# Value weights of a graph-attention kernel by two levels of Strassen's algorithm

## The chip, the cores and the metric

The kernel runs on one core of a Trainium2 chip. The core has five engines that work side by side: TensorE (PE in the profile; PEld is its loading of weights), VectorE (DVE), ScalarE (ACT), GpSimd (POOL) and SyncE (SP, which here only issues DMAs). Each engine runs its instructions in the order in which the program gives them, and waits in that order. Matrix products go to PSUM, eight banks of 512 float32 columns; POOL does not touch PSUM here, so results are moved out ("evicted") by DVE or ACT. The metric is device time in microseconds, the median of three runs.

## The reference, cut to what matters

Two graph layers over x (128 graphs of 64 nodes, 768 features), all in float32:

```python
# layer 0
u = einsum('bld,bmd->blm', x, x) / sqrt(768)
attn = softmax(u) * adj, renormalized
h_left, h_self, h_right = x @ W_left.T + b_left, x @ W_self.T + b_self, x @ W_right.T + b_right
ctx = upper(attn) @ h_left + diag(attn)[..., None] * h_self + lower(attn) @ h_right
x = layernorm(x + relu(layernorm(ctx) * gamma + beta))
# layer 1, 12 heads of 64
q, k, v = x @ Wq + bq, x @ Wk + bk, x @ Wv + bv
scores = q k^T / 8 + beta * adj, masked where adj is 0
x = layernorm(x + softmax(scores) @ v)
```

The change is in `v = x @ Wv + bv` alone.

## The kernel before, in words

The 8192 tokens go in 16 blocks of 512 (`NBLK`). The loop over n works on layer 1 of block n and layer 0 of block n + 1 in turns, in five stages whose order PE follows: the left and right parts of layer 0 of the next block (from block 3 on together, `both_sides`), its self part (`self_part`), the values of block n (`values`), and three projections of queries and keys (`projected`, hg = 0, 1, 2). Smaller work (attention of layer 0, scores, weighted sums, the context pieces of 8 matmuls) is put between products by hooks: a dictionary from a place in a stage to functions that are called there. Element-wise work waits in three queues, `first`, `urgent` and `lazy`; after each product `step` takes an item from them, and a call with `light` set takes none of the ordinary DVE items (those without a kind). The whole loop is scheduled by hand: the order of the program is the order on each engine.

Every projection is done by one level of Strassen's algorithm in Winograd's form: the 512 x 768 block and the 768 x 768 matrix are cut in four, and seven products replace eight. `combined` and `combined4` form the sums of tokens S (POOL), `prepare` formed the sums of weights at the start and stored them in DRAM. `seven` runs the seven products, in the order 1, 2, 6, 5, 7, 4, 3, for two halves j of the tokens: 14 places, three matmuls of 128 x 128 weights by 384 columns in each, so 42 for a stage. The products gather in PSUM tiles X (1, 6, 7, 4) and Y (2; 5, 3), two of each, and are evicted on the way (14 evictions). `by_tokens` is this with the tokens as PE's stationary operand and a weight piece of 128 x 384 as the moving one, loaded by SP into the ring `wst` (19 buffers).

From block 3 on, `both_sides` uses two levels (`nested`): each of the seven products is again done by seven, over the left and right matrices side by side (384 columns). A pair of numbers, first level and second level, names a product. `ORDER2` is the first-level order 7, 1, 2, 6, 5, 4, 3; the order on PE is 7.1 7.2, then for each i: i.6 i.5 i.7, the next one's 1 and 2, i.4 i.3. Products 2, 5, 4 and 3 of the second level take two matmuls, the others one. Each product of the second level is evicted by itself (49 evictions): `middle` takes it to a temporary U, `final` to its quarter of the output, in both cases adding what is there already. At first-level product 5, POOL adds c22 to c21, the bias to c12 and c12 to c22, quarter by quarter (lines 450 to 458). `second_level` forms the second-level sums of tokens of one product by four POOL instructions in a tile q (lines 341 to 344) of a pool of two buffers; `blk["S"]["deep"]` holds the first two, formed in `combined` for layer 0 of blocks from 3 on. `deepened` makes the 63 second-level matrices of left and right in blocks 0 and 1 and stores them in `lr_d`.

The stage of values, in which the change lies, begins when the self part ends. Its hooks: place 0, the last sum of tokens and the loads for later transposes; places 1, 3, 5, 7, the four context pieces, each 8 matmuls and two DVE instructions on them; place 6, six DVE transposes of 512 columns put in `urgent` (`turned`, line 310); places 9 and 13, small steps of a layernorm. The sums of tokens for the values are formed in the self part, place 11.

Of the kernel before, what the change touches and what calls it, by code (L numbers as in the profile page):

```python
# [11 lines left out]
F32 = mybir.dt.float32  # L12
AF = mybir.ActivationFunctionType
ALU = mybir.AluOpType
# [3 lines left out]
P = 128  # L18
# [28 lines left out]
MATRICES = (1, 2, 8, 3, 9, 5, 7, 4, 6)  # L47
DEEP = 3
# [3 lines left out]
def gnn_two_layers(ctx: ExitStack, tc, x, adj, wl, bl, ws, bs, wr, br, gamma, beta,  # L52
# [9 lines left out]
    s2_p = ctx.enter_context(tc.tile_pool(name="s2", bufs=2))  # L62
# [3 lines left out]
    wst = ctx.enter_context(tc.tile_pool(name="wst", bufs=19))  # L66
# [218 lines left out]

    def transposed(src, xT, t):

        for c0 in range(0, KC, 3):
            ps = ps_mm.tile([P, 4, P], F32, tag="mm", name="ps_x")
            for c in range(3):  # L290
                nc.tensor.transpose(ps[:, c, :], src[:, c0 + c :: KC], ident)  # L291
            nc.scalar.copy(xT[:, c0 : c0 + 3, t * P : (t + 1) * P], ps[:, 0:3, :])
# [132 lines left out]
    def nested(width, sums, load, multiply, view, C, bias0, bias1, hooks):  # L425
# [9 lines left out]

        def part(i, q):
            return bias0(q[1]) if i == 1 else old[i][q] if i in old else None

        def taken(i, q, ps, dst, add):
            if add is None:  # L440
                nc.scalar.copy(dst, view(ps))
            else:
                nc.vector.tensor_tensor(dst, view(ps), add, ALU.add)  # L443
# [16 lines left out]
        def sub(i, j):  # L460
            for place in range(28):
                if place * 49 // 28 == len(done):
                    for f in hooks.get(place, ()):
                        f()
# [6 lines left out]
            multiply(F[i], W[i], j, ps)  # L471
# [13 lines left out]

            step(len(done) > 8, j in (5, 1, 4))
# [4 lines left out]
        for k, i in enumerate(ORDER2):  # L491
            after = ORDER2[k + 1] if k + 1 < len(ORDER2) else None
            if after:
                F[after], W[after] = sums(after), load(after)
            for j in (6, 5, 7):
                sub(i, j)
            if after:
                sub(after, 1)
                sub(after, 2)
            for j in (4, 3):  # L500
                sub(i, j)
# [118 lines left out]
    def both_sides(n, hooks):  # L620
# [6 lines left out]
        def sums(i):  # L627
            return blk["S"]["deep"].get(i) or second_level(blk["S"][i])

# [7 lines left out]
        def multiply(F, w, j, ps):  # L637
            f, last = F
            fs = [(f[j], w[j])]
            if j in (2, 5, 4, 3):  # L640
                fs.append((last[{2: 1, 5: 2, 4: 2, 3: 3}[j]], w[8 if j in (2, 4) else 9]))
            for k, (a, b) in enumerate(fs):
                nc.tensor.matmul(ps, lhsT=a, rhs=b, start=(k == 0 and j in (1, 2, 5)), stop=(k == len(fs) - 1),  # L643
                                 skip_group_check=True)

        def view(ps):
# [4 lines left out]
        nested(HALF, sums, load, multiply, view, C,  # L651
               lambda b: bias_lr[:, :, b * QUAD : (b + 1) * QUAD],
               lambda b: bias_lr[:, :, HALF + b * QUAD : HALF + (b + 1) * QUAD], hooks)
# [112 lines left out]
    def values(n, hooks={}, stay=False):  # L766
# [12 lines left out]
        by_tokens("v", blocks[n]["S"], last, None, hooks)  # L779
# [240 lines left out]
    for n in range(NBLK):  # L1020
# [12 lines left out]
        for i, (when, hooks, place) in zip(ORDER2, ((0, val, 2), (0, val, 8), (0, qk[0], 8), (0, qk[1], 6),  # L1033
                                                    (0, qk[2], 6), (1, own, 3), (1, val, 3))):
            if when == n:
                begin, steps = deepened(i)
                at(hooks, place, begin)
                at(hooks, place + 3, lambda i=i, steps=steps: urgent.extendleft([(("d", i), *f) for f in reversed(steps)]))

# [14 lines left out]
        if not last:  # L1054
            if n > 0:
# [29 lines left out]
                def sums1():  # L1085
                    settle(("t1", n))
                    blocks[n]["S"] = combined(blocks[n]["xT"])

                at(own, 11, sums1)
# [47 lines left out]
        else:  # L1137
            transposed1(n)
            at(qk[0], 9, lambda: later(("m", n), *mask(n), queue=urgent))
# [142 lines left out]
```

## Time and profile before

| what | time, us |
|---|---|
| median of three runs | 2923.98 (2923.8 to 2925.47) |
| profiled execution | 2923.8, its span 2922.1 |
| PE busy | 2872.4 (98% of the span) |
| DVE busy | 1979.6 (68%) |
| ACT busy | 1120.4 (38%) |
| POOL busy | 732.2 (25%) |
| DMA | 613.18 MB, 210 GB/s over the span |

The page's first part gives each engine's busy time; the chain that ended last follows the work back from the last instruction. In a timeline a line is start, length, engine, source line, operation, output and inputs, shape, number of instructions merged, and in brackets how long the engine had been idle and for what. The granted PE clock is full in all slices of the span.

### The profile page before, as it was taken

To read this page: it belongs to the slowest core of one execution; us is meant where nothing else is said; L and a number is where in the kernel's file an instruction comes from. 1 tells how busy PE (TensorE), PEld (TensorE's weight loads), DVE (VectorE), ACT (ScalarE), POOL (GpSimd) and SP (SyncE) were. 2 spreads that over 40 slices of the span, in tenths; PEclk is the share of its full clock that TensorE was granted. 3 is DMA by queue.
4 is the path that set the end of the run, shared out by engine and by line. 5 is a ranking of instruction groups with operands and counts; after the bars stand their busy time and mean duration, and the time that the engine had idled before them with its cause. 6 is when DMAs were issued, how large, how long until landed. Compare 5 with 4: busy or idle time off the path is not lost.

```text
span 2922.1 us, 49871 instructions
## 1 busy us (share of the span) xinstructions
PE 2872.4 (98%) x17578; PEld 1931.7 (66%) x17578; DVE 1979.6 (68%) x3973; ACT 1120.4 (38%) x2107; POOL 732.2 (25%) x879
## 2 busy tenths in 40 slices
PE   9999999999999999999999999999999999999997
PEld 5658566585665857657576675766757567585685
DVE  6778777676676766757667576766767667676655
ACT  0005224354243443434444334343434424354255
POOL 3133123213042140412405123051230512314110
PEclk9999999999999999999999999999999999999999
DMA  9788877859577595875958669486694956849443
GB/s 340 231 272 272 251 214 202 243 143 286 153 207 238 160 274 149 226 220 167 270 145 246 195 181 267 137 269 174 184 260 138 285 160 195 246 139 288 140 127 100
DMA packets 440662, 613.18 MB, mean 210 GB/s; under 512 B 53584, under 2 KB 416720, under 8 KB 440416
## 3 DMA queue, kind: packets, MB, share of 16 engines
q1 hardware_dynamic: 362960, 495.93, 56.5%
q10 hardware_dynamic: 60848, 44.05, 8.0%
q0 software_dynamic: 16608, 70.01, 6.6%
q8 instruction: 143, 2.34, 0.3%
q14 instruction: 103, 0.84, 0.1%
HBM read 539.43 MB, written 77.27 MB: 211 GB/s over the span
## 4 chain that ended last, share of the span: by engine, by line
PE 93%; ACT 3%; POOL 2%; DVE 1%; issue 1%; DMA 0%; POOLq 0%; SPq 0%; ACTq 0%
PE ps_X L389 36%; PE ps_Y L389 27%; PE ps_Y L643 11%; PE ps_X L643 10%; PE ps_ctx L682 3%; ACT eT L853 2%; PE sc L833 2%; PE ps_y L882 2%; PE u L532 2%; POOL q L342 1%; ACT L853 1%; ACT uqk L801 1%; PE ps_x L291 0%; POOL q L341 0%; POOL q L343 0%
## 5 line engine op out<-in xcount | busy, mean ns | idle before, releaser
L389 PE MATMUL ps_X<-xT,wqk 128*128 128x256 f32 x1728 | 395.8, 381 | 9.5 <-ACT uqk L801 9.5
L853 ACT ACTIVATE eT<-s 32x256 f32<-32x256 f32 x768 | 317.8, 414 | 172.4 <-DVE s L862 162.4
L389 PEld LDWEIGHTS ps_X<-xT,wqk 128*128 128x128 f32 x1728 | 325.8, 190 | 67.0 <-ACT uqk L801 16.2
L322 POOL TENSOR_TENSOR S<-hT 128x768 f32<-128x768 f32 x16 | 28.9, 1807 | 1132.7 <-PE ps_Y L389 1102.1
L389 PE MATMUL ps_Y<-S,wqk 128*128 128x256 f32 x1152 | 264.3, 379 | 0.0
L687 ACT ACTIVATE unused<-o 128x768 f32<-128x768 f32 x60 | 50.6, 844 | 499.6 <-DVE o L684 346.1
L389 PEld LDWEIGHTS ps_Y<-S,wqk 128*128 128x128 f32 x1152 | 218.9, 190 | 29.8
L443 DVE TENSOR_TENSOR lr<-ps_Y,u_deep 128x384 f32<-128x384 f32 x273 | 152.1, 557 | 109.1 <-PE ps_Y L643 83.4
L643 PE MATMUL ps_Y<-wlr,q 128*128 128x384 f32 x546 | 208.5, 491 | 0.0
L389 PE MATMUL ps_X<-wv,xT 128*128 128x384 f32 x576 | 195.5, 489 | 0.0
L801 ACT ACTIVATE uqk<-ps_X,bq 128x256 f32<-128x256 f32 x144 | 68.1, 473 | 325.0 <-PE ps_X L389 323.9
L809 DVE TENSOR_TENSOR q<-ps_Y,uqk 128x256 f32<-128x256 f32 x144 | 61.0, 424 | 177.5 <-ACT uqk L801 89.3
L389 PE MATMUL ps_X<-ws,hT 128*128 128x384 f32 x540 | 179.2, 486 | 0.0
L643 PE MATMUL ps_X<-wlr,q 128*128 128x384 f32 x364 | 151.0, 497 | 14.6 <-POOL q L342 6.0
L389 PEld LDWEIGHTS ps_X<-wv,xT 128*128 128x128 f32 x576 | 108.0, 190 | 80.4 <-issue 8.4
L892 DVE SCALAR_TENSOR_TENSOR o<-ps_y,rz,o 128x64 f32<-128x64 f32 x720 | 154.7, 278 | 6.4
L443 DVE TENSOR_TENSOR u_deep<-ps_X,lr 128x384 f32<-128x384 f32 x195 | 107.5, 551 | 68.2 <-PE ps_X L643 66.6
L389 PEld LDWEIGHTS ps_X<-ws,hT 128*128 128x128 f32 x540 | 102.5, 190 | 71.4
L643 PEld LDWEIGHTS ps_Y<-wlr,q 128*128 128x128 f32 x546 | 101.6, 190 | 67.2
L420 DVE TENSOR_TENSOR u<-ps_X,bv 128x384 f32<-128x384 f32 x96 | 53.4, 557 | 132.5 <-PE ps_X L389 132.5
L389 PE MATMUL ps_X<-S,wqk 128*128 128x256 f32 x576 | 138.2, 385 | 0.0
L389 PE MATMUL ps_Y<-xT,wqk 128*128 128x256 f32 x576 | 135.6, 385 | 0.0
(258 smaller groups left out, 5471.6 us busy)
## 6 DMA issues: line engine op xcount, KB each, us to landing
wlr<-lr_d SPq DMA_DIRECT2D x819, 192.0 KB, 3.5
wqk<-qk_d SPq DMA_DIRECT2D x672, 192.0 KB, 2.4
wv<-d_v SPq DMA_DIRECT2D x192, 192.0 KB, 2.7
ws<-d_s SPq DMA_DIRECT2D x180, 192.0 KB, 5.8
wv<-in_L_gnn_Wv_dram SPq DMA_DIRECT2D x144, 192.0 KB, 4.1
ws<-in_L_gnn_W_self_dram SPq DMA_DIRECT2D x135, 192.0 KB, 5.4
xa<-in_x_dram SPq DMA_DIRECT2D x64, 384.0 KB, 5.3
sq<-in_x_dram ACTq DMA_DIRECT2D x56, 384.0 KB, 7.7
```

Source lines behind the costliest of these rows:

```text
L389: nc.tensor.matmul(ps, lhsT=a, rhs=b, start=(c == 0 and i in (1, 2, 5)), stop=(c == len(fs) - 1), skip_group_check=True)
L420: recent["u"] = evicted[nm] = nc.vector.tensor_tensor(u, ps, bias[nm][:, b * HALF : (b + 1) * HALF], ALU.add)
L443: nc.vector.tensor_tensor(dst, view(ps), add, ALU.add)
L532: nc.tensor.matmul(u[g * L : (g + 1) * L, t, :], lhsT=xT[:, c, tok], rhs=xT[:, c, tok], start=(c == 0), stop=(c == KC - 1))
L643: nc.tensor.matmul(ps, lhsT=a, rhs=b, start=(k == 0 and j in (1, 2, 5)), stop=(k == len(fs) - 1), skip_group_check=True)
L682: nc.tensor.matmul(ps[g * L : (g + 1) * L, 0:HALF], lhsT=blk["aT"][:, t, g * L : (g + 1) * L], rhs=blk["lr"][t][:, g, cols], start=True, s ...
L801: nc.scalar.activation(u, ps, AF.Identity, bias=bias["qk"[j]][:, c : c + 1])
L809: nc.vector.tensor_tensor(dst, ps, part, ALU.add)
L833: nc.tensor.matmul(sc[r][g * L : (g + 1) * L, t, c, :], lhsT=q[rows, c, tok], rhs=k[rows, c, tok], start=True, stop=True)
L853: nc.scalar.activation(e[to[0], :, to[1]], pairs[rows, :, cols], AF.Exp)
L882: nc.tensor.matmul(y[r, h][cols, t, c, :], lhsT=eT[rows, 2 * h + t, c, cols], rhs=v[rows, 2 * h + t, g, hg + c * HC, :], start=True, stop= ...
L892: nc.vector.scalar_tensor_tensor(res[:, r, c, hg, :], ps[:, t, c, 0:HD], rz[:, t, c : c + 1], res[:, r, c, hg, :], ALU.mult, ALU.add)
```

## The change

From block 3 to block 14 the values are computed by two levels too; blocks 0 to 2 and the last keep one level.

- `deepened_values` makes the second-level matrices of Wv in block 2 and stores them in `v_d`, in five pairs to a first-level product (`PAIRS`). A column half is cut by the parity of the head, so the loads read runs of 64 columns.
- `nested` is made general: `applied` does the one or two matmuls of a product; `places` is 28 for both sides and 14 for values. With 14, all evictions are DVE's, and ordinary DVE items of the queues run only after a second-level product 7.
- The pool of q has three buffers instead of two, the ring of weights 17 instead of 19. In both users of `nested`, the second-level sums of products 4 and 3 are now formed together, before 5.6; those of the others one product ahead, as before.
- The sums of tokens for the values are formed at place 10 instead of 11 of the self part, with the two first sets of second-level sums among them.
- The second half of the values' bias is replaced by its difference to the first half at block 3, and loaded anew for the last block.

```diff
...
 MATRICES = (1, 2, 8, 3, 9, 5, 7, 4, 6)
+PAIRS = ((1, 2), (8, 6), (5, 9), (7, 4), (3,))
 DEEP = 3
...
     s_p = ctx.enter_context(tc.tile_pool(name="s_p", bufs=1))
-    s2_p = ctx.enter_context(tc.tile_pool(name="s2", bufs=2))
+    s2_p = ctx.enter_context(tc.tile_pool(name="s2", bufs=3))
     l0 = ctx.enter_context(tc.tile_pool(name="l0", bufs=1))
...
     tmp = ctx.enter_context(tc.tile_pool(name="tmp", bufs=2))
-    wst = ctx.enter_context(tc.tile_pool(name="wst", bufs=19))
+    wst = ctx.enter_context(tc.tile_pool(name="wst", bufs=17))
     st = ctx.enter_context(tc.tile_pool(name="st", bufs=2))
...
         return begin, [(partial(formed, 0),), (partial(formed, 1),), (end, "gap")]
+    v_d = tc.dram_tile([7, len(PAIRS), P, 2, QUAD], F32, name="v_d")
+    def deepened_values(i):
+        src, w = pieces["v"][i], {}
+        place = {m: v_d[i - 1, k, :, j, :].rearrange("p (j d) -> p j d", d=HD)
+                 for k, pair in enumerate(PAIRS) for j, m in enumerate(pair)}
+        def half(k, h):
+            return src[:, k, :].rearrange("p (j r d) -> p r j d", r=2, d=HD)[:, h]
+        def heads(a):
+            return a.rearrange("p (j d) -> p j d", d=HD)
+        def begin():
+            for k in range(2):
+                w[k] = wst.tile([P, 2, QUAD], F32, tag="w", name="w_deep")
+                for h in range(2):
+                    nc.sync.dma_start(out=heads(w[k][:, h, :]), in_=half(k, h))
+            for m, k, h in ((1, 0, 0), (2, 1, 0), (8, 2, 0), (3, 1, 1), (9, 2, 1)):
+                nc.gpsimd.dma_start(out=place[m], in_=half(k, h))
+        def formed():
+            b11, b12, b21, b22 = (w[k][:, h, :] for k in range(2) for h in range(2))
+            for out, a, b in ((b11, b12, b11), (b12, b22, b12), (b22, b22, b11), (b21, b21, b22)):
+                nc.vector.tensor_tensor(out, a, b, ALU.subtract)
+        def end():
+            for m, k, h in ((5, 0, 0), (7, 0, 1), (4, 1, 0), (6, 1, 1)):
+                nc.gpsimd.dma_start(out=place[m], in_=heads(w[k][:, h, :]))
+        return begin, [(formed,), (end, "gap")]
...
-    def nested(width, sums, load, multiply, view, C, bias0, bias1, hooks):
+    def applied(F, w, j, ps):
+        f, last = F
+        fs = [(f[j], w[j])]
+        if j in (2, 5, 4, 3):
+            fs.append((last[{2: 1, 5: 2, 4: 2, 3: 3}[j]], w[8 if j in (2, 4) else 9]))
+        for k, (a, b) in enumerate(fs):
+            nc.tensor.matmul(ps, lhsT=a, rhs=b, start=(k == 0 and j in (1, 2, 5)), stop=(k == len(fs) - 1),
+                             skip_group_check=True)
+    def nested(width, S, load, view, C, bias0, bias1, hooks, places):
...
+        def sums(i):
+            return S["deep"].get(i) or second_level(S[i])
         def part(i, q):
...
         def taken(i, q, ps, dst, add):
-            if add is None:
+            if add is None and places == 28:
                 nc.scalar.copy(dst, view(ps))
+            elif add is None:
+                nc.vector.tensor_copy(dst, view(ps))
             else:
...
         def sub(i, j):
-            for place in range(28):
-                if place * 49 // 28 == len(done):
+            for place in range(places):
+                if place * 49 // places == len(done):
                     for f in hooks.get(place, ()):
...
             ps = (X if j in (1, 6, 7, 4) else Y)[i][:, 0:width]
-            multiply(F[i], W[i], j, ps)
+            applied(F[i], W[i], j, ps)
             if j == 1:
...
                 final(i, (0, 1), ps, U[i, 2])
-            step(len(done) > 8, j in (5, 1, 4))
+            step(places == 14 or len(done) > 8, j in (5, 1, 4) if places == 28 else j != 7)
...
             if after:
-                F[after], W[after] = sums(after), load(after)
+                W[after] = load(after)
+            for later_one in (ORDER2[k + 1 :] if i == 5 else (after,) if i != 4 and after else ()):
+                F[later_one] = sums(later_one)
             for j in (6, 5, 7):
...
-        def sums(i):
-            return blk["S"]["deep"].get(i) or second_level(blk["S"][i])
         def load(i):
...
-        def multiply(F, w, j, ps):
-            f, last = F
-            fs = [(f[j], w[j])]
-            if j in (2, 5, 4, 3):
-                fs.append((last[{2: 1, 5: 2, 4: 2, 3: 3}[j]], w[8 if j in (2, 4) else 9]))
-            for k, (a, b) in enumerate(fs):
-                nc.tensor.matmul(ps, lhsT=a, rhs=b, start=(k == 0 and j in (1, 2, 5)), stop=(k == len(fs) - 1),
-                                 skip_group_check=True)
         def view(ps):
...
                        for a in range(2) for b in range(2)} for m in range(2) for n_ in range(2)}
-        nested(HALF, sums, load, multiply, view, C,
+        nested(HALF, blk["S"], load, view, C,
                lambda b: bias_lr[:, :, b * QUAD : (b + 1) * QUAD],
-               lambda b: bias_lr[:, :, HALF + b * QUAD : HALF + (b + 1) * QUAD], hooks)
+               lambda b: bias_lr[:, :, HALF + b * QUAD : HALF + (b + 1) * QUAD], hooks, 28)
...
-        by_tokens("v", blocks[n]["S"], last, None, hooks)
+        def load(i):
+            w = {}
+            for k, pair in enumerate(PAIRS):
+                two = wst.tile([P, 2, QUAD], F32, tag="w", name="wv2")
+                nc.sync.dma_start(out=two[:, 0 : len(pair), :], in_=v_d[i - 1, k, :, 0 : len(pair), :])
+                w.update({m: two[:, j, :] for j, m in enumerate(pair)})
+            return w
+        def heads(a):
+            return a.rearrange("p (j d) -> p j d", d=HD)
+        if n < DEEP or stay:
+            by_tokens("v", blocks[n]["S"], last, None, hooks)
+        else:
+            C = {(m, h): {(a, k): v[:, 2 * m + a, k, h * HC : (h + 1) * HC, 0:HD]
+                          for a in range(2) for k in range(2)} for m in range(2) for h in range(2)}
+            nested(QUAD, blocks[n]["S"], load, lambda ps: heads(ps[:, 0:QUAD]), C,
+                   lambda k: pairs(bias["v"][:, 0:HALF])[:, k], lambda k: pairs(bias["v"][:, HALF:D])[:, k], hooks, 14)
         if not stay:
...
                 at(hooks, place + 3, lambda i=i, steps=steps: urgent.extendleft([(("d", i), *f) for f in reversed(steps)]))
+        for i, (hooks, place) in zip(ORDER2, ((left, 3), (left, 9), (right, 3), (right, 9), (own, 2), (own, 7), (val, 5))):
+            if n == 2:
+                begin, forms = deepened_values(i)
+                at(hooks, place, begin)
+                at(hooks, place + 2, lambda i=i, forms=forms: urgent.extendleft([(("dv", i), *f) for f in reversed(forms)]))
+        if n == DEEP:
+            settle("dv")
+            at(left, 0, lambda: nc.vector.tensor_tensor(bias["v"][:, HALF:D], bias["v"][:, HALF:D],
+                                                        bias["v"][:, 0:HALF], ALU.subtract))
...
                     settle(("t1", n))
-                    blocks[n]["S"] = combined(blocks[n]["xT"])
-                at(own, 11, sums1)
+                    blocks[n]["S"] = combined(blocks[n]["xT"], n)
+                at(own, 11 if n < DEEP else 10, sums1)
                 at(val, 0, lambda: combined4(blocks[n]["S"]))
...
             transposed1(n)
+            at(qk[0], 0, lambda: nc.sync.dma_start(out=bias["v"], in_=bv.partition_broadcast(P)))
             at(qk[0], 9, lambda: later(("m", n), *mask(n), queue=urgent))
...
```

## The prediction

> **What bounds the kernel now.** I read the page's busy shares first, then the chain that ended last, then the merged chain in order of time, and last the timelines of one block (the one that runs from about 1969 to 2149 us).
>
> ```profile
> PE 2872.4 (98%) x17578; PEld 1931.7 (66%) x17578; DVE 1979.6 (68%) x3973; ACT 1120.4 (38%) x2107; POOL 732.2 (25%) x879
> PE 93%; ACT 3%; POOL 2%; DVE 1%; issue 1%; DMA 0%; POOLq 0%; SPq 0%; ACTq 0%
> L389 PEld LDWEIGHTS ps_X<-xT,wqk 128*128 128x128 f32 x1728 | 325.8, 190 | 67.0 <-ACT uqk L801 16.2
> ```
>
> PE is 98% busy and is 93% of the chain, so time is passes times their price. Each f32 matmul is two records ("passes"): the 42 matmuls of a block's self part are 84 records.
>
> The merged chain gives the price (start, length, what):
>
> ```profile
> 30.82 7.74 PE ps_X L389 x24
> 240.99 5.18 PE ps_X L389 x24
> ```
>
> 24 passes over 384 columns take 7.74 us, 322.5 ns each; 24 over 256 take 5.18, 215.8 each. So 106.7 ns per 128 columns, and by that line a pass over 192 columns costs 322.5 - 1.5 x 106.7 = 162.5 ns.
>
> The value stage of the block, in PE's timeline:
>
> ```profile
> 1995.24 2.10 PE L389 MATMUL ps_X<-wv,xT 128*128 128x384 f32 x6
> 1997.26 1.51 PE L682 MATMUL ps_ctx<-lr,aT 128*64 128x384 f32 x8
> 1998.70 2.20 PE L389 MATMUL ps_X<-wv,xT 128*128 128x384 f32 x6
> ...
> 2028.88 2.75 PE L389 MATMUL ps_X<-xT,wqk 128*128 128x256 f32 x12
> ```
>
> It lasts 2028.88 - 1995.24 = 33.64 us without a wait: 84 passes are 27.09, and the four context pieces the other 6.55.
>
> How the nested form behaves is seen where it already runs, in the both-sides stage. First the handing of X between PE and DVE (all engines' timeline):
>
> ```profile
> 2111.28 1.22 DVE L862 TENSOR_TENSOR s<-s,mx 128x1024 f32<-128x1024 f32 x1
> 2111.29 1.53 POOL L342 TENSOR_TENSOR q<-q,S 128x128 f32<-128x128 f32 x1
> 2112.42 0.55 DVE L443 TENSOR_TENSOR u_deep<-ps_X,lr 128x384 f32<-128x384 f32 x1
> 2113.07 0.88 PE L643 MATMUL ps_X<-wlr,q 128*128 128x384 f32 x2 [0.46 <-POOL q L342]
> 2113.99 0.56 DVE L443 TENSOR_TENSOR u_deep<-ps_X,lr 128x384 f32<-128x384 f32 x1 [1.02 <-PE ps_X L643]
> ```
>
> The wait of 0.46 is put down to POOL, but PE moves 0.10 us after the eviction ends at 2112.97. DVE starts 0.27 after the stream ends (2113.07 + 0.645 = 2113.72, then 2113.99). So X is lost to PE for 0.27 + eviction + 0.10. Second, POOL's queue at product 5 (POOL's timeline):
>
> ```profile
> 2125.49 0.99 POOL L457 TENSOR_TENSOR lr<-lr,bias_lr 128x384 f32<-128x384 f32 x1 [0.29 <-DVE rz L888]
> 2126.57 0.99 POOL L458 TENSOR_TENSOR lr<-lr,lr 128x384 f32<-128x384 f32 x1
> 2127.52 0.46 POOL L341 TENSOR_TENSOR q<-hT 128x128 f32<-128x128 f32 x1
> 2128.05 0.46 POOL L342 TENSOR_TENSOR q<-q,hT 128x128 f32<-128x128 f32 x1
> 2128.47 0.73 POOL L343 TENSOR_TENSOR q<-hT 128x256 f32<-128x256 f32 x1
> 2129.15 0.46 POOL L344 TENSOR_TENSOR q<-hT,q 128x128 f32<-128x128 f32 x1
> 2129.56 1.00 POOL L450 TENSOR_TENSOR lr<-lr 128x384 f32<-128x384 f32 x1
> ```
>
> A set of second sums takes 2129.56 - 2127.52 = 2.04, say 2.08 us. An add takes 0.46 at 128 columns, 0.73 at 256, 1.00 at 384: 0.59 at 192, or 0.56 from start to start and 0.67 where the next needs its result.
>
> **The change, part by part.** I write 5.1 for first-level product 5, second-level product 1.
>
> *PE.* In blocks 3 to 14 (12 blocks) 42 matmuls become 7 x (3 x 1 + 4 x 2) = 77, over 192 columns: 154 passes x 162.5 ns = 25.03 us, with the context pieces 31.58. That is 2.06 a block less, if nothing waits. A single product is 0.325, a double one 0.65. Bounds of a pass: 161 (half of 384's) and 190, the recorded length of a weight load; I stay at 162.5, since the 64-column passes of u come every 3.02/96 = 31 ns with loads recorded at 138, so a load's record is longer than what it holds PE for.
>
> "TensorE: Matmul & The Clock Gate", section "Back-to-back issue gap", speaks against: it says that a stream's spacing is set by loads and matmuls together, 81 ns at 128 columns where the matmul alone gives 56. No run here shows it at 192. Were those 25 ns added to each of 154 passes, an estimate from that page, a block would cost 3.9 us and the twelve 46 us more.
>
> *DVE.* 14 evictions of 384 columns become 49 of 192, on PSUM: 0.42 at 256 and 0.56 at 384 give 0.36, and 0.27 from start to start (384 columns: 0.46 for 0.55). 49 x 0.27 = 13 us against 14 x 0.46 = 6.4, beside PE; what counts is the four places where PE waits for one:
> - i.6 to i.7: X is away 0.27 + 0.36 + 0.10 = 0.73, the cover is i.5, 0.65. 0.08 each; the context pieces stand in that gap for 7, 1, 2 and 6, so three are left, some of them hidden in waits below: 0.1.
> - 3.7 to 3.4: nothing lies between. 0.7. In the both-sides stage a transpose of 0.6 covers the same gap.
>
> *POOL, at products 5 and 4.* This is the dear part. Before 5.6 is issued, the new code queues the second sums of 4 and 3 one after the other, and the adds of c21, c12, c22 of 5.6, 5.7, 5.4, 5.3 stand behind both. With 0 at the end of 5.1's stream: PE has 5.2, 6.4, 6.3, 5.6, 5.5, 5.7, 4.1, 4.2, 5.4, 5.3, 4.6, 4.5 (eight of 0.65, four of 0.325: 6.5) before 4.7. DVE evicts twice for 6.7 (from -0.05), then does the first of the six hT transposes, which are queued in place 6 and may now run only at a step of a seventh product: 0.49 to 1.51. 5.1 is evicted until 1.87, 5.2 until 2.14. POOL: c21 of 5.1 from 1.97, the bias add at 2.53, c22 3.20 to 3.77, sums of 4 to 5.85, of 3 to 7.93, c21 of 5.6 to 8.52. Only then can DVE evict 4.6, which adds that c21: 8.62 to 8.98, and 4.7 starts at 9.08 in place of 6.5: 2.6 lost (0.4 of it already at 4.6, which needs the sums of 4). Behind, six adds of 5.7 and 5.4 bring c12 for 3.6 at 12.66; DVE ends 3.6 at 13.12 and 3.7 starts 13.22 where PE could at 12.65: 0.6 lost.
>
> Bounds: adds 0.46 to 0.73 (four stand in the first sum: -0.5 to +0.6, and the 0.6 behind goes away or doubles); without the transpose ahead -1.0; second sums 2.08, or 2.36 by the mean of the four groups on the page. "SBUF — State Buffer", section "Who interferes with whom", says that VectorE instructions with two SBUF inputs shut GpSimd out, and those with one do not. The 1.53 of q beside L862 above agrees; value evictions read one operand from PSUM, so by the rule 2.08 holds, and 2.36 would be 0.56 a block, 7 us in all, more.
>
> *POOL, elsewhere.* Five more sets of sums and the two early ones in the self part (first one needed at 7.6, by POOL's timeline at 1988.13 + 1.85 + 1.95 + 2.2 = 1994.1, PE there at 1996.2) run ahead of use: nothing. The third buffer takes POOL's waits for PE out of the both-sides stage, but PE's waits there end 0.10 after an eviction, as shown: nothing. Its adds come 2.1 us later behind two sets of sums: c21 of 5.6 at 2132.7, wanted 2135.6: nothing.
>
> *DMA.* Values load 28 x 196.6 + 7 x 98.3 KB = 6.2 MB in place of 4.1, 196 GB/s over 31.6 us; the both-sides stage moves 234 to 348. 17 buffers are 3.4 groups ahead, 12 us, against landings of 8.2 at most: hidden. For the both-sides weights 17 instead of 19 buffers delays a load to when the second next is issued now; the tightest is the third of product 3: 2130.63 + 6.5 = 2137.1, used at 2138.6. Hidden, with 1.5 us to spare.
>
> *Once.* In block 2 the values' matrices are made: 28 loads on SP, 28 subtractions of 0.37 on DVE, 63 DMAs on POOL of some 0.73 (the row of lr_d): 46 us of POOL. One group of nine stands among the adds of product 5 in the both-sides stage, up to 6.6 us, with some 2.5 to spare there: I take 4, bounds 0 and 12. The bias subtraction and its reload at the end: nothing, SP is far ahead.
>
> *Sum.* Waits 0.1 + 0.7 + 2.6 + 0.6 = 4.0 against 2.06: +1.9 a block, x12 = +22.5, +4 once. The profiled execution took 2923.8 (span 2922.1), 0.2 under the median of 2923.98: 2923.8 + 26.5 = 2950.
>
> **The rivals.**
> - *POOL is in time, and it is faster.* The POOL waits (3.2) must fall below 2.06 - 0.8 = 1.26. With none left: (0.8 - 2.06) x 12 = -15, +4: 2913, or 2909 without the cost once. For it: with cheap adds and no transpose ahead, 2 of the 3.2 go. Against: two sums alone are 4.2 of the 6.5 us that PE gives. With 1.3 us of waits it is a draw.
> - *Weight loads set the pace.* Passes at 190: +4.2 a block; PE's cover at POOL grows by 1.1, so POOL waits fall to about 1.5: 38.0 a block, +52: 2980. Against: u's passes.
> - *Weights come late in the both-sides stage.* If landings of 8.2 met the third load, 0.2 a block; if a whole us is lost, 13 blocks give +13: 2963. Against: 1.5 us to spare.
>
> **How the numbers follow.** What a measurement of this kernel can tell from no change is about 0.2%, 6 us. My forecast 0.60, late weights 0.08, slow passes 0.06: slower 0.74. POOL in time 0.18: faster. Gains and waits cancel: 0.08. The forecast's own range is 2934 (transpose not ahead, nothing once) to 2965 (sums 2.36, once 12). The range takes in the lower half of the draw and most of POOL in time: 2910 to 2970; half of the fastest cases and the slow passes are left out.
>
> **What would show it.** Right: value passes 162 ns apart; the stage 35 to 36 us; PE waits of 2 to 3 us at 4.6 and 4.7, ended by DVE's eviction that itself waited for a POOL add behind two sets of sums; 0.7 at the end. Wrong: passes at 175 or more; POOL's second sums of 4 done before 5.1; waits on DMA; time lost in the self or projection stages, which I leave as they are.

## The result, and the profile after

The kernel after takes 2963.00 us (median of four runs, 2962.36 to 2966.14) where the kernel before takes 2924.43 (2923.8 to 2925.47): a ratio of 1.0133, 95% interval [1.0121, 1.0145]. It is slower by 38.6 us. The profiled execution took 2962.93, with a span of 2960.9, which is 38.8 more than before's 2922.1.

The page's busy shares and the chain that ended last, of the kernel after:

```profile
PE 2876.8 (97%) x18418; PEld 2040.8 (69%) x18418; DVE 2094.3 (71%) x4422; ACT 1119.3 (38%) x2107; POOL 1020.4 (34%) x1422
PE 87%; POOL 4%; ACT 3%; DMA 3%; DVE 2%; issue 1%; SPq 0%; POOLq 0%; DVEq 0%; ACTq 0%
```

PE fell from 93% to 87% of the chain; POOL, DMA and DVE have what it lost. (PE's busy time did not fall, although there are fewer columns to stream: a record of 192 columns is 326 ns long and the next starts 162.5 ns after it, so a short wait between two of them still counts as busy. Of a value stage of 35.46 us, 33.49 count as busy.) What PE waits for, in the waits of the kernel after (in total, times, longest):

```profile
PE ps_X L467 <- DVE u_deep L493: 26.6, 39, 2.0
PE ps_X L467 <- DMA wlr<-lr_d: 7.6, 1, 7.6
PE ps_X L467 <- issue: 7.0, 29, 0.8
PE ps_y L939 <- DVE eT L914: 3.8, 3, 1.9
PE ps_X L424 <- DMA ws<-d_s: 1.0, 1, 1.0
```

Before, the first of these waits was 2.8 us in 13 times and the second wasn't there. From the starts of the stages on PE's timeline the 38.8 us lie here:

| where | before | after | difference |
|---|---|---|---|
| values, blocks 3 to 13, each | 33.64 | 35.46 | +1.82, x11 = 20.0 |
| values, block 14 | 33.64 | 34.45 | +0.8 |
| block 2, both sides of the next block | 56.53 | 72.32 | +15.8 |
| block 2, self part of the next block | 27.09 | 29.26 | +2.2 |
| block 1, left part of the next block | 33.63 | 35.28 | +1.6 |
| late weights here and there, to block 14 | | | +1.1 |
| behind the last block's projections | | | -2.7 |

So there are two nearly equal halves: twelve value stages, +20.8, and what happens once in block 2, +18.0. The rest sums to nothing: +1.6 and +1.1, less 2.7. The gain at the end lies behind the last ACT instruction, where no product runs: from its end to the end of the span it is 7.0 us before and 4.2 after. It is 3.8 to 4.2 in every run below that makes the matrices and 7.0 in the two that do not; what sets it is open.

**The value stage.** PE's timeline of block 10, whose stage begins at 2027.86 (start, length, ..., idle before):

```profile
2031.39 0.49 PE L467 MATMUL ps_Y<-wv,xT 128*128 128x192 f32 x2
2031.72 0.49 PE L467 MATMUL ps_X<-wv,q 128*128 128x192 f32 x2
2032.05 0.49 PE L467 MATMUL ps_X<-wv,xT 128*128 128x192 f32 x2
...
2054.20 0.56 PE L467 MATMUL ps_X<-wv,q 128*128 128x192 f32 x2
2054.60 0.56 PE L467 MATMUL ps_Y<-wv,q 128*128 128x192 f32 x2
2055.00 0.49 PE L467 MATMUL ps_Y<-wv,xT 128*128 128x192 f32 x2
2056.86 0.59 PE L467 MATMUL ps_X<-wv,q 128*128 128x192 f32 x2 [1.37 <-DVE u_deep L493]
...
2060.87 0.59 PE L467 MATMUL ps_X<-wv,q 128*128 128x192 f32 x2
2061.91 0.92 PE L467 MATMUL ps_X<-wv,S 128*128 128x192 f32 x4 [0.45 <-DVE u_deep L493]
2062.66 0.81 PE L467 MATMUL ps_Y<-wv,q 128*128 128x192 f32 x4
2063.32 1.03 PE L424 MATMUL ps_X<-xT,wqk 128*128 128x256 f32 x4
```

The first three lines give the price: two passes every 0.325 us, 162.5 ns each. The line at 2056.86 is 4.7, behind 1.37 us of waiting; the one at 2061.91 is 3.4, behind 3.7 (1.04 us from start to start, where a product of two passes takes 0.325: 0.72 lost, of which the bracket shows 0.45). The stage ends at 2063.32, 35.46 after its start.

Why 4.7 is late is on POOL's and DVE's timelines (5.1's stream ends on PE at 2048.01):

```profile
2049.95 0.60 POOL L500 TENSOR_TENSOR v<-v 128x192 f32<-128x192 f32 x1 [8.08 <-DVE u_deep L493]
2050.51 0.57 POOL L507 TENSOR_TENSOR v<-v,bv 128x192 f32<-128x192 f32 x1
2051.15 0.59 POOL L508 TENSOR_TENSOR v<-v 128x192 f32<-128x192 f32 x1
2051.70 0.46 POOL L376 TENSOR_TENSOR q<-xT 128x128 f32<-128x128 f32 x1
...
2053.76 0.46 POOL L376 TENSOR_TENSOR q<-S 128x128 f32<-128x128 f32 x1
...
2055.82 1.14 POOL L500 TENSOR_TENSOR v<-v 128x192 f32<-128x192 f32 x2
```

```profile
2048.55 1.08 DVE L345 STREAM_TRANSPOSE hT<-sq 128x512 f32<-128x512 f32 x1
2049.56 0.31 DVE L493 TENSOR_TENSOR u_deep<-ps_X,v 128x192 f32<-128x192 f32 x1
...
2056.44 0.36 DVE L493 TENSOR_TENSOR u_deep<-ps_X,v 128x192 f32<-128x192 f32 x1 [1.41 <-POOL v L500]
```

A transpose stands ahead of 5.1's eviction (2049.56); POOL then does the adds, the sums of 4 from 2051.70, those of 3 from 2053.76, and only at 2055.82 the adds of 5.6, for which DVE's eviction of 4.6 has waited 1.41 us.

**Block 2.** PE's timeline in the both-sides stage:

```profile
497.40 0.88 PE L467 MATMUL ps_X<-wlr,q 128*128 128x384 f32 x2 [0.78 <-issue]
505.87 1.62 PE L467 MATMUL ps_X<-wlr,S 128*128 128x384 f32 x2 [7.58 <-DMA wlr<-lr_d]
507.28 2.34 PE L467 MATMUL ps_Y<-wlr,S 128*128 128x384 f32 x4
509.46 1.45 PE L467 MATMUL ps_X<-wlr,hT 128*128 128x384 f32 x4
...
541.92 0.91 PE L467 MATMUL ps_X<-wlr,q 128*128 128x384 f32 x2 [1.98 <-DVE u_deep L493]
```

PE stands 7.58 us for one weight load. SP's timeline shows that the loads behind it were issued late, and SP's waits between 484 and 502 us for what:

```profile
480.33 8.86 SPq L683 DMA_DIRECT2D wlr<-lr_d  x9
489.66 10.28 SPq L306 DMA_DIRECT2D w_deep<-in_L_gnn_Wv_dram  x4
500.11 14.97 SPq L683 DMA_DIRECT2D wlr<-lr_d  x18
```

```profile
SPq L306 <- DMA sq<-x1d: 6.7, 1, 6.7
```

Four loads of the values' pieces took SP 10.28 us, 6.7 of it in one wait for `sq<-x1d`, a transfer that ScalarE's queue had issued. The weights that PE needed at 498 were issued from 500.11 on. In this program the loads of SP and ScalarE report to the same eight counters (semaphores 100 to 105, 107 and 108 in the packed trace). One `sq<-x1d` was issued at 490.84 on counter 103 and landed at 499.56; the fourth load of pieces, also on 103, waits for that counter and was issued at 499.57. The runs below that make the matrices in the same place by the same pieces have this wait too (5.5, 5.9 and 5.3 us). No run gives the two queues counters of their own.

The passes at 505.87 to 509.46 ran at half speed, and the granted clock shows it (windows of the kernel after: stretch, length, busy time of PE, PEld, DVE, ACT and POOL, then granted clock, DMA share, GB/s):

```profile
495.00:505.00 10.00, 2.51 (x8) 0.91 (x6) 4.44 (x9) 0.00 (x0) 2.23 (x4) 0.86 1.16 230
505.00:509.00 4.00, 3.13 (x5) 1.85 (x6) 0.56 (x1) 2.32 (x6) 0.00 (x0) 0.50 0.88 270
509.00:520.00 11.00, 9.14 (x89) 5.50 (x88) 6.36 (x13) 4.30 (x11) 4.72 (x9) 1.00 1.06 278
```

Six passes took 509.46 - 505.87 = 3.59 us in place of 6 x 0.3225 = 1.94: another 1.65. The Trainium skill, "TensorE: Matmul & The Clock Gate", section "Part 1: The HAM clock gate", has a window of about 3.4 us, half clock after one without work and full clock after a busy one; these rows agree with it.

The account of the 15.8: the weight wait 7.6, the clock 1.65, waits of PE for DVE 2.7 (1.98 of it at 541.92) and for eT 1.9, 1.2 of the kind "issue" (0.78 of it at 497.40), less the 1.3 of waits that this stage has in the kernel before, make 13.7; 2 us lie in gaps too short for a line. The 1.98 is the mechanism that the prediction had: from 538.52 DVE does four subtractions for 2.88 us, from 537.86 POOL issues four DMAs for 2.22 between its adds, and DVE's eviction at 541.32, for which PE waits, comes when both have just ended (POOL's add behind those DMAs at 541.18); which of the two held it is not separated.

### The profile page after: what moved, and what is told of

Its sections match the earlier page's. It is cut to its first block, busy times and chain, and to the rows that moved or that the text cites. A ratio compares the mean times of both kernels' runs of the same rounds, so it can differ in the third digit from the quotient of the medians.

```text
span 2960.9 us, 53414 instructions
## 1 busy us (share of the span) xinstructions
PE 2876.8 (97%) x18418; PEld 2040.8 (69%) x18418; DVE 2094.3 (71%) x4422; ACT 1119.3 (38%) x2107; POOL 1020.4 (34%) x1422
## 4 chain that ended last, share of the span: by engine, by line
PE 87%; POOL 4%; ACT 3%; DMA 3%; DVE 2%; issue 1%; SPq 0%; POOLq 0%; DVEq 0%; ACTq 0%
PE ps_X L424 29%; PE ps_Y L424 21%; PE ps_Y L467 15%; PE ps_X L467 14%; PE ps_ctx L722 3%; ACT eT L910 2%; PE sc L890 2%; PE ps_y L939 2%; PE u L584 2%; POOL q L377 1%; DMA wv<-v_d 1%; DVE u_deep L493 1%; ACT L910 1%; POOL q L378 1%; POOL q L376 1%
## 5 line engine op out<-in xcount | busy, mean ns | idle before, releaser
L357 POOL TENSOR_TENSOR S<-xT 128x768 f32<-128x768 f32 x16 | 28.9, 1806 | 339.5 <-DVE xT L345 267.7
L467 PEld LDWEIGHTS ps_X<-wlr,q 128*128 128x128 f32 x364 | 64.8, 189 | 82.2 <-POOL q L378 19.0
L424 PE MATMUL ps_Y<-ws,S 128*128 128x384 f32 x360 | 121.0, 486 | 0.0
```

What stands on the lines that cost most here:

```text
L357: nc.gpsimd.tensor_tensor(s1, a21, a22, ALU.add)
L424: nc.tensor.matmul(ps, lhsT=a, rhs=b, start=(c == 0 and i in (1, 2, 5)), stop=(c == len(fs) - 1), skip_group_check=True)
```

## The experiments

My theory on seeing the result: the value stage is what was forecast (POOL's order, the transposes ahead of evictions, 3.7 to 3.4), and block 2's cost comes from making the matrices, mostly from the DMAs. Rivals: that DVE, not POOL, is what makes 4.7 late; that the smaller ring of weights or the new order of sums in the both-sides stage causes part of it; that the 256-byte pieces are all of block 2's cost.

**The matrices are not made**, and the values read other weights, those of `lr_d`.

```diff
-            if n == 2:
+            if n < 0:
...
-                nc.sync.dma_start(out=two[:, 0 : len(pair), :], in_=v_d[i - 1, k, :, 0 : len(pair), :])
+                nc.sync.dma_start(out=two[:, 0 : len(pair), :], in_=lr_d[i - 1, k, :, 0 : len(pair), :])
```

> The changed kernel without deepened_values: the 28 loads, 28 subtractions and 63 POOL DMAs of block 2 are left out, and the values load the same number of bytes from lr_d (the matrices of left and right) instead of v_d, so the values are computed from other weights. Theory (the making of the matrices costs some 18 us once, because its pieces of 256 bytes make all landings slow and SP's queue stands still behind them): about 2945 us, the wait of 7.6 us on wlr in block 2 and the slow passes behind it gone, the value stage unchanged at 35.5 us. Rival (the ring of 17 buffers or the third pool buffer brings the waits of block 2): about 2963, waits in block 2 as they are.

Measured: 2951.88 (2948.66 to 2954.37), ratio 1.0091 [1.0076, 1.0106]. The both-sides stage of block 2 is back at 56.52, its self part at 27.09, the left part of block 1 at 33.64; the value stage stays 35.46. So the +18.0 of block 2 come from making the matrices. The +1.6 of block 1 do not: that stage runs before the making begins, and the next two runs, which make the matrices, do not have it (33.63 and 33.64). The time came down by 11.1 only (the profiled execution by 14.0), because other weights came late in this run (block 11's self part 28.83, PE waits of 1.8 for `ws` in all) and because the 2.8 at the program's end went back, too.

**The sums of 4 one product earlier**, those of 3 as before:

```diff
-            for later_one in (ORDER2[k + 1 :] if i == 5 else (after,) if i != 4 and after else ()):
+            ahead = ORDER2[k + 1 : k + 3] if i == 6 else ORDER2[k + 2 :] if i == 5 else (after,)
+            for later_one in ahead if i != 4 and after else ():
```

> The changed kernel with the second-level sums of product 4 formed together with those of product 5, one product earlier, so that only the sums of 3 stand ahead of the adds of product 5 on POOL. Theory (POOL's queue at product 5 is what PE waits for): c21 of 5.6 comes 2.1 us earlier, the wait at 4.7 falls from 2.35 to about 0.4, that at 3.7 stays near 0.6 because PE is earlier too: the stage 33.5 us in place of 35.46, 12 blocks, about 2939 us. Rival (DVE's 49 evictions and transposes are what PE waits for): the stage stays within 0.3 of 35.46, about 2963.

Measured: 2947.79 (2942.1 to 2948.56), ratio 1.0074 [1.0059, 1.0089]; the stage 33.97, 1.49 a block less. The wait at 4.7 is gone from the list, and 3.4's is untouched (PE's timeline of the same block, from 4.6 on):

```profile
2043.50 0.59 PE L467 MATMUL ps_X<-wv,q 128*128 128x192 f32 x2
2043.97 0.59 PE L467 MATMUL ps_Y<-wv,q 128*128 128x192 f32 x2
2044.39 0.49 PE L467 MATMUL ps_Y<-wv,xT 128*128 128x192 f32 x2
2044.76 0.59 PE L467 MATMUL ps_X<-wv,q 128*128 128x192 f32 x2
...
2049.82 0.92 PE L467 MATMUL ps_X<-wv,S 128*128 128x192 f32 x4 [0.45 <-DVE u_deep L493]
```

POOL's order was the cause of most of the wait; DVE alone, with the same work, does not make it. The stage is 0.5 longer than expected. Twelve blocks of 1.49 would be 17.9 us and the time fell by 15.2: late weights make two both-sides stages 58.06 and 59.74 long in this run.

**The transposes two places later** (place 8, behind 5.1's eviction):

```diff
-                at(val, 6, turn0)
+                at(val, 6 if n < DEEP else 8, turn0)
```

> The changed kernel with the six hT transposes queued at place 8 of the value stage in place of 6 (blocks from 3 on), so that the first one runs after 5.7 and none stands ahead of the eviction of 5.1. Theory (the transpose ahead of 5.1 delays POOL's queue by about 1.2 us): the wait at 4.7 falls from 2.35 to 1.1, the stage to 34.3, about 2949 us. Rival (POOL's queue is long because of its work alone, and the transpose costs nothing, or its cost comes back later in the first projection stage): within 4 us of 2963.

Measured: 2951.07 (2947.81 to 2957.81), ratio 1.0092 [1.0077, 1.0107]; the stage 34.49, 0.97 less. In block 10, 4.7 starts 7.88 us after 5.1's stream in place of 8.85: the prediction had "without the transpose ahead -1.0". Some transposes now fall into the next projection, which becomes 0.2 shorter, not longer. The two edits each take away part of one wait, so their gains cannot be added.

**The kernel before with the small rings**: three buffers of q, 17 of weights, and the new order of sums in the both-sides stage.

```diff
-    s2_p = ctx.enter_context(tc.tile_pool(name="s2", bufs=2))
+    s2_p = ctx.enter_context(tc.tile_pool(name="s2", bufs=3))
...
-    wst = ctx.enter_context(tc.tile_pool(name="wst", bufs=19))
+    wst = ctx.enter_context(tc.tile_pool(name="wst", bufs=17))
...
-                F[after], W[after] = sums(after), load(after)
+                W[after] = load(after)
+            for later_one in (ORDER2[k + 1 :] if i == 5 else (after,) if i != 4 and after else ()):
+                F[later_one] = sums(later_one)
```

> The kernel before with three buffers for the second-level sums, 17 buffers of weights, and the new order of those sums in both_sides, the values by one level as before. Theory (these are hidden in both_sides): 2924 us, within 3 us. Rival (17 buffers make the weights of both_sides late): slower by 0.2 us or more in each of 13 blocks, 2927 or more, with waits on wlr.

Measured: 2927.93 (2925.86 to 2933.6), ratio 1.0013 [1.0004, 1.0023]: some 3 us. Two of the thirteen both-sides stages are longer (57.87 and 57.30 for 56.53), with a wait that the kernel before does not have:

```profile
PE ps_Y L645 <- DMA wlr<-lr_d: 1.1, 1, 1.1
```

The first values start 1.0 later, too, but not in the kernel after (193.75 for 193.68), whose ring is 17 as well. The other eleven both-sides stages are within 0.2 of 56.53, so the new order of sums costs nothing; that the waits are for weight loads speaks for the ring of 17, which was not run by itself. The time is the rival's; 0.2 us in each of 13 blocks it is not.

**Whole rows.** The matrices are read and written as rows of 384 columns (1536 bytes); the parity is taken by the access pattern of the matmul and of the subtractions. In each group of a first-level product that leaves two loads for four and two stores for nine DMAs of POOL.

```diff
         def begin():
             for k in range(2):
-                w[k] = wst.tile([P, 2, QUAD], F32, tag="w", name="w_deep")
-                for h in range(2):
-                    nc.sync.dma_start(out=heads(w[k][:, h, :]), in_=half(k, h))
-            for m, k, h in ((1, 0, 0), (2, 1, 0), (8, 2, 0), (3, 1, 1), (9, 2, 1)):
-                nc.gpsimd.dma_start(out=place[m], in_=half(k, h))
+                w[k] = wst.tile([P, HALF], F32, tag="w", name="w_deep")
+                nc.sync.dma_start(out=w[k], in_=src[:, k, :])
...
         def end():
-            for m, k, h in ((5, 0, 0), (7, 0, 1), (4, 1, 0), (6, 1, 1)):
-                nc.gpsimd.dma_start(out=place[m], in_=heads(w[k][:, h, :]))
+            for k in range(2):
+                nc.gpsimd.dma_start(out=v_d[i - 1, k], in_=w[k])
...
-            for k, pair in enumerate(PAIRS):
+            for pair, rows in (((1,), src[:, 0, :]), ((2, 3), src[:, 1, :]), ((8, 9), src[:, 2, :]),
+                               ((4, 6), v_d[i - 1, 1]), ((5, 7), v_d[i - 1, 0])):
...
```

> The changed kernel with the values' second-level matrices made and read by whole rows: the heads' parity is taken by the access patterns of DVE and PE, so block 2 issues 14 loads and 14 stores of 1536-byte rows instead of 28 loads, 28 stores and 35 copies in DRAM by pieces of 256 bytes; the five matrices that are quarters of stored pieces are not copied. Theory (the cost once is the small pieces and their number in SP's and POOL's queues): both_sides of block 2 back from 72.3 to 57 us, the value stage 35.46 as it was, about 2948 us. Rival (any making of the matrices beside both_sides costs this, or PE reads the strided rows slower): both_sides above 65, or value passes above 162.5 ns and a stage over 35.7.

Measured: 2954.07 (2951.48 to 2955.97), ratio 1.0098 [1.0085, 1.0112]; the both-sides stage of block 2 64.54 in place of 72.32, the value stage 35.41 (rows of two parities cost PE nothing). Half right: 7.8 us go, 8.0 stay. SP has no long stop now, but its loads of weights still come too slowly; SP's timeline and PE's in the same stretch:

```profile
490.12 1.39 SPq L299 DMA_DIRECT2D w_deep<-in_L_gnn_Wv_dram  x2
491.83 20.83 SPq L674 DMA_DIRECT2D wlr<-lr_d  x18
```

```profile
500.27 0.89 PE L458 MATMUL ps_X<-wlr,S 128*128 128x384 f32 x2 [1.02 <-DMA wlr<-lr_d]
501.65 1.74 PE L458 MATMUL ps_Y<-wlr,S 128*128 128x384 f32 x4 [0.50 <-DMA wlr<-lr_d]
```

The length of the pieces and the number of DMAs change together here, so this run does not say which of the two counts.

**POOL's order, more of it**: the sums of 4 early as above, and the four adds of c12 to c22 put off until the adds of 5.7 (and of 5.3) are done.

```diff
...
+        def added():
+            while waiting:
+                q = waiting.pop(0)
+                nc.gpsimd.tensor_tensor(c22[q], c22[q], c12[q], ALU.add)
...
                 nc.gpsimd.tensor_tensor(c12[q], c12[q], bias1(q[1]), ALU.add)
-                nc.gpsimd.tensor_tensor(c22[q], c22[q], c12[q], ALU.add)
+                waiting.append(q)
+                if q == (0, 1):
+                    added()
```

> The changed kernel with the sums of 4 one product earlier and the four adds of c12 to c22 put off behind the adds that products 4 and 3 wait for. No work is taken away. Theory (POOL's order at product 5 makes all waits beyond those of the hand-over of X): c21 of 5.6 comes at 5.8 us after 5.1 and c12 of 5.3 at 9.2, both before they are wanted; the stage falls from 35.46 to 32.7, of which 0.7 is 3.7 to 3.4, and 12 blocks give 2963 - 33 = 2930 us. Rival (with POOL out of the way DVE's evictions and transposes set the pace): the stage no better than 33.9, as in the run with the sums of 4 early.

Measured: 2941.92 (2941.07 to 2949.1), ratio 1.0065 [1.0049, 1.008]; the stage 34.00, not 32.7. With the sums of 4 early nothing more is to be had from this change of POOL's order: the stage was 33.97 without it. (The run above is longer by 5.7 us in its profiled execution, mostly by its late weights.) Against the 31.58 of the passes 2.4 remain. Block 14 tells a part of them: its instructions on DVE and POOL are those of block 13 but for four transposes, and its stage is 33.07. So 0.93 are the transposes; 0.72 are 3.7 to 3.4, which an eviction ends; the rest lies in gaps too short for the list of waits, and that evictions make those, too, is not shown.

**All three**: this order of POOL, the transposes at place 8, whole rows.

> The changed kernel with POOL's new order, the transposes queued at place 8, and the matrices made by whole rows. Theory: the stage 32.5 us against 33.64 before, 13 us won in twelve blocks; the cost once near 0; 17 buffers cost some 3 us as measured in the kernel before: 2913 to 2917 us, faster than the kernel before. Rival (the gains overlap, or the waits turn up in the projections, which then get three transposes): 2924 or more.

Measured: 2929.70 (2924.38 to 2935.86), ratio 1.0015 [1.0006, 1.0024]. The stage is 33.65, as long as the one-level stage before (33.64): the 2.06 us that the passes save are all spent on waits, and the gain of 13 us that was expected is not there. The both-sides stage of block 2 has 63.62, still 7.1 too much.

**The matrices made elsewhere**: as the last, but in the projections of blocks 1 and 2 and the values of block 2, where no nested stage runs.

```diff
-        for i, (hooks, place) in zip(ORDER2, ((left, 3), (left, 9), (right, 3), (right, 9), (own, 2), (own, 7), (val, 5))):
-            if n == 2:
+        for i, (when, hooks, place) in zip(ORDER2, ((1, qk[0], 8), (1, qk[1], 6), (1, qk[2], 6), (2, val, 3),
+                                                    (2, qk[0], 8), (2, qk[1], 6), (2, qk[2], 6))):
+            if when == n:
```

> As the run with all three edits, with the values' matrices made in the projection stages of blocks 1 and 2 and one in the value stage of block 2, instead of beside both_sides and the self part of block 2. The same instructions, moved. Theory (what is left of the cost once, 7 us at both_sides of block 2, is the place: PE's weights there fill the queue): both_sides of block 2 at 56.5 instead of 63.6, about 2922 us. Rival (the making costs the same wherever it stands): some other stage of blocks 1 or 2 longer by 7, about 2930.

Measured: 2925.53 (2922.71 to 2930.77), ratio 1.0002 [0.9993, 1.0011]. The both-sides stage of block 2 is 58.35, the projections are no longer than in the last run, and no other stage of blocks 1 and 2 is longer by more than 0.5, but for block 1's left part. That one has 35.18, where the last run had 33.63; it runs before the making begins, here too, so its 1.6 are not the making's. The place where the matrices were made was the larger part of what the whole rows had left; 1.8 of it remain, so the 56.5 that was expected is not reached.

**The gap filled**: as the last, and the first product of the next projection is issued between 3.7 and 3.4.

```diff
+            if len(done) == 47 and 47.5 in hooks:
+                hooks[47.5]()
             done.append((i, j))
...
+            if n >= DEEP:
+                val[47.5], rest0 = projected(n, 0, qk[0], {})
...
```

> As the run with the matrices made elsewhere, with the first product of the first projection (3 matmuls, 1.3 us) issued between 3.7 and 3.4 of the values. Theory (PE stands 0.72 us at 3.4 for the eviction of 3.7, and only that): the value stage and the first projection together 0.6 us shorter, 12 blocks: 7 us less than without, about 2915. Rival (the wait comes back at the second product of the projection, which needs the X tile of 3.4): the same as without, about 2922.

Measured: 2919.11 (2915.85 to 2922.44), ratio 0.9975 [0.9965, 0.9985]. Stage and first product together are 34.26, of which the product is 1.29: 32.97 for the values in place of 33.65, and 0.1 more in the projection (62.37 for 62.27). So -0.58 a block, where 0.6 was expected.

**The transposes out of the stage's hard part**: as the last, with `turn0` at place 10 and the scores of the next block one place later.

```diff
-                at(val, 6 if n < DEEP else 8, turn0)
+                at(val, 6 if n < DEEP else 10, turn0)
...
-                at(qk[0], 4, scores0)
+                at(qk[0], 4 if n < DEEP else 5, scores0)
```

> As the run with the gap filled, with the hT transposes queued at place 10 (two in the value stage, four in the first projection) and the scores of layer 0 one place later. Theory (each transpose in the value stage delays evictions that PE waits for, 0.3 us each): 0.3 to 0.5 us a block less, about 2910 us. Rival (DVE's work is only moved and PE waits for hT or for the layernorm in the projection): the same or more, 2915 or above.

Measured: 2914.76 (2912.31 to 2916.44), ratio 0.9959 [0.9945, 0.9973]: faster than both kernels, with -0.25 a block where 0.3 to 0.5 was expected. PE's timeline of block 10 around the gap, 3.7 first, and the page's PE line:

```profile
2025.24 0.59 PE L462 MATMUL ps_X<-wv,q 128*128 128x192 f32 x2
2025.67 1.46 PE L887 MATMUL ps_X<-xT,wqk 128*128 128x256 f32 x6
2026.97 0.81 PE L462 MATMUL ps_X<-wv,S 128*128 128x192 f32 x4
```

```profile
PE 2863.7 (98%) x18418; PEld 2045.1 (70%) x18418; DVE 2086.8 (72%) x4422; ACT 1121.6 (39%) x2107; POOL 987.4 (34%) x1373
```

The values cost 32.72 a block, 0.92 under the one level; 1.14 over the passes. Twelve blocks of 0.92 and 0.11 in the projections are 12.4 us, and the program's end gives 3.0 more (4.0 for 7.0); the once-costs, block 1's 1.6 and late weights bring that to the measured 10.3. Without the end's 3.0, which no product has a part in, some 7 us would be left, by estimate.

## Why the prediction was right and wrong

The forecast was 2950 within 2910 to 2970, slower with 0.74. Slower it is, and 2963.0 lies in the range. The two halves of its sum went differently: +22.5 for the twelve stages was measured as +20.8, and +4 once was measured as +18.0 in block 2. (By its own terms, 4.0 less 2.06 in twelve blocks, the first half should have read +23.3.) That the range held is in part luck: the 18.0 lie above the bound of 12 for that term, and the 2.7 at the program's end, which nobody forecast, offset the 1.6 of block 1 and the late weights. It is chance, too, that the rival "Weights come late in the both-sides stage" names 2963: behind block 2 these stages are within 0.2 of 56.53.

- **The pass, 162.5 ns**: right, shown above. The rival "weight loads set the pace" falls, and with it the 25 ns for each pass worked out from the Trainium skill, "TensorE: Matmul & The Clock Gate", section "Back-to-back issue gap": the loads of these products are still recorded at 190 ns, yet the passes come every 162.5.
- **POOL at products 5 and 4**: right nearly to the step. From the end of 5.1's stream, c21 of 5.1 was to start at 1.97 and did at 1.94 (2049.95); c21 of 5.6 was to be done at 8.52 and was at about 8.4 (2055.82 and half of 1.14); 4.7 was to start at 9.08 and did at 8.85, where the passes alone need 6.5. So 2.35 lost against 2.6. The adds of 192 columns took 0.57 to 0.60 (0.59 taken), the evictions 0.36 (0.36), the second sums 2.06 (2.08).
- **3.6 to 3.7**: 0.44 lost for 0.6 (from 4.7 to 3.7 the passes need 3.58, measured 4.01). **3.7 to 3.4**: 0.72 for 0.7, and 0.7 again by what filling the gap gave. **i.6 to i.7 elsewhere**: with other small gaps 0.4 for 0.1. All waits 3.9 for 4.0.
- **The transposes** cost a stage 1.0 us: block 14, which has none and which I counted like the others, has 34.45 for 35.46, and the run that moved them has 34.49 in the other blocks.
- **"POOL is in time, and it is faster"**: its draw was put at 1.3 us of POOL waits. With POOL's order mended the stage still had 2.4 us of waits and 34.00 us, over the 33.64 of one level. The rival counted what is not POOL's at 0.8; the transposes on DVE had 0.93 that it left out, and small gaps most of the rest, part of it covered until then by POOL's longer wait.
- **DMA "hidden"**: of 17 buffers I wrote "Hidden, with 1.5 us to spare". That failed by a little: some 3 us in the run with the small rings, 2 of them as late loads in two stages. The margin was worked out on the landings of one block, 8.2 us at most; over that run they reach 9.1.
- **The term that was mis-sized is "Once"**: "I take 4, bounds 0 and 12". Its mechanism, subtractions on DVE and DMA issues on POOL among the adds of product 5, is there and costs about 2.5 (PE's 2.7 of waits for DVE in that stage, less 0.2 before). What I left out is SP: "SP is far ahead" was said of the bias, and the 28 loads of the pieces were counted on SP without asking what they wait for. They stood in front of the both-sides weights in a queue that is only as far ahead as its ring, and held them for 6.7 us behind a transfer of another queue; the wait, the clock after it and the slow landings behind it are most of the 18.0, above my upper bound. Leaving the making out brought all of it back, and moving it to other stages, with whole rows, left 1.8 in the both-sides stage and 0.4 in the self part.

What stays open: which of piece length and number of DMAs makes the difference of 7.8 us between the two ways of making the matrices; why block 1's left part has 1.6 more in the kernel after and the last three runs and not in the others; and the 1.9 us for eT, which appears with the making in the both-sides stage (also with whole rows) and not when it is moved out.

## What to carry to other kernels

Work that is done once must be costed in the queue it is put in, not by its share of the run: ask for each DMA what it waits for before it is issued, and which load with a due time stands behind it. Fewer operations on the bound engine are worth only what the evictions of the smaller pieces leave over: here a gain of 2.06 us a block met 3.9 us of waits, and 0.92 of it came back only when POOL's queue was put in order of need, the transposes were moved off, and another product was put where nothing covered an eviction. Price first the place where nothing lies between a product and the next that needs its bank.

## What the runs showed of the hardware

- A load on SP's queue waited 6.7 us for a transfer that ScalarE's queue had issued, and all that stood behind it on SP waited with it.
- After a wait of 7.58 us PE ran at a granted clock of 0.50 for 3.6 us. In block 1 it fell after less: two waits for eT of 0.75 and 1.18 us, 0.70 us of 64-column products between them, were there before and after alike, yet in the kernel after the clock fell (0.57 from 321 to 325 us, 1.00 before; six passes took 3.7 us in place of 2.0). It fell in the last three runs, too, and in none of the first seven. The same waits gave two clocks, so their length alone does not decide. PE's lines behind the waits, after first:

```profile
321.38 3.85 PE L424 MATMUL ps_Y<-wl,S 128*128 128x384 f32 x6
```

```profile
321.32 2.20 PE L389 MATMUL ps_Y<-wl,S 128*128 128x384 f32 x6
```

- Landings beside the small pieces: the median of the weight loads issued between 483 and 492 us of the kernel after is 7.3 us, and 3.9 at the same place of the kernel before (481 to 490). Two `sq<-x1d` of 384 KB were issued in the first of these stretches and none in the second, so that the pieces alone make the loads slow is not shown. The lines of the DMA view, after first:

```profile
wlr<-lr_d SPq DMA_DIRECT2D x5, 192.0 KB, 7.3
```

```profile
wlr<-lr_d SPq DMA_DIRECT2D x11, 192.0 KB, 3.9
```
- Four subtractions of 192 columns on DVE took 1.53 us at 510.13 and 2.88 at 538.52. POOL had DMAs to issue in both stretches and adds in the second alone. Four more at 528.88 took 2.20, beside sums on POOL and no DMA of its queue. What slowed them was not isolated.
